# Four stacked graph layers on one core: streamed weights moved to ScalarE's DMA queue, weight combinations spread over phase 1, q's bias folded into a copy, and the planner's order made anew

## The chip, the cores and the metric

The kernel runs on one core of one Trainium2 chip. The metric is the device time of one execution in microseconds. Before the change it is 2448.98 us, the median of two runs (2447.59 and 2450.36).

## What is computed

The input is x (128 graphs of 64 nodes, 512 features, float32) and one 64x64 weighted adjacency per graph. Four layers follow, each as x + layer(relu(layernorm(x))), all in float32:

```python
# layer 0: hypergraph convolution, H = (adj != 0), twice, with a layer norm between
h = layer_norm(relu(hypergraph_conv(h, adj, W1, b1)))      # 512 -> 1024
y = hypergraph_conv(h, adj, W2, b2) + x                    # 1024 -> 512
# layer 1: attention from one score per node, s = (h @ w) @ a
A = exp(lrelu(tanh((s_i + s_j) / 8) * 8)) * adj; A = A / rowsum(A) * rowsum(adj)
out = A @ h @ w
# layer 2: q, k, v attention, masked by adj
weight = adj * exp(q @ k^T); out = (weight / rowsum(weight)) @ v
# layer 3: three hops, H = sum over k of T^k h @ Wk[k] + bk[k], out = relu(H)
T = adj * exp(lrelu(sj + si + ab)); T = T / rowsum(T)
```

## The kernel before

The 8192 nodes are 16 groups of 4 tiles of 128 nodes (two graphs per tile, so a tile's adjacency is block diagonal, buffer tag `bd`). There are two phases. Phase 1 runs layers 0 and 1 over all groups and stores the result to DRAM (`xm`, L845). Phase 2 loads it again and runs layers 2 and 3. The weights of phase 1 lie in SBUF; in phase 2 that memory holds the weights of layer 2 and, in three slots `wf`, pieces of layer 3's weights that are streamed from DRAM.

Matrix products with weights are 2x2 Strassen products with seven multiplications: `seven` (L605 on) multiplies, copies the first partial sum out of PSUM by ScalarE into a buffer U (L612), makes two further sums by VectorE (L614, L616), and hands four results to an `emit` function. `strassen` (L626 on) is used in phase 1, with its matmuls at L644. Layer 2's products (matmuls at L882) go through `seven` too: q first, with the product of Wq and Wk folded into one matrix. `emit_q` gives the four parts of q their bias `gb_c`: the part without U by two ScalarE activations (L896), the three others by a GpSimd addition U + bias (L902) and then a VectorE addition of PSUM (L903). v is made likewise (L936 on GpSimd, L938 on VectorE).

Layer 3 uses two levels of Strassen, so 7 x 7 block products of 128x128, each summed over three hops (matmuls at L1074). The combined weights of each outer product f (7 of them) are made once in phase 1 by `setup_w3` (L517 on): for each f and each hop k (21 calls) it loads blocks of Wk (L525), subtracts on GpSimd (L529, and L533 to L535) and stores the factors to DRAM in `fac` (four stores per call, L539). In phase 2, `product` (L1049 on) reads each f in two parts (768 KB for four blocks, 576 KB for three) into a `wf` slot by a DMA from SyncE (L1066), 14 per group, 224 in all. Results are copied by ScalarE (L1083) or added by VectorE (L1089) into Z, combined by GpSimd (L1097 to L1101), and added to x by VectorE (L1105), then stored (L1109).

Layers 2 and 3 need transposed activations. `transposed` (L588 on) does it with a ScalarE copy (L592), a DMA transpose issued by SyncE (L593), and a ScalarE copy back (L594). Layer norms are VectorE statistics (L553, L554), GpSimd arithmetic (L555, L556, L561) and one ScalarE activation (L574).

The order of all work is made by a planner at build time (`Graph`). Every operation is given an engine, a cost in us, what it reads and writes, and a priority; `run` simulates the engines, and at each step takes the operation that can start first, by priority among equals. A result is ready for others after the operation's cost and the engine's latency (`LATENCY`, 2.0 for DMAs). The priority is `G.prio` plus the shift of the part (`AT`, set by `part`); `step` raises it as work is laid down, by a factor of the layer (`STRETCH`), and a group starts `PERIOD1` or `PERIOD2` after the one before. Where the planner sees TensorE idle for over 0.5 us it puts in filler matmuls (L1141). Each engine then runs its own queue strictly in the planned order, with semaphores for the dependences. All DMAs are issued by SyncE: `dma` makes an operation of engine "SP" with a cost of its size over 380 KB/us, at least 0.34.

Of the kernel before, what the change touches and what calls it, by code (L numbers as in the profile page):

```python
# [35 lines left out]
class Op:  # L36
    __slots__ = ("eng", "cost", "fn", "prio", "bufs", "npre", "succ", "ready", "seq")


class Graph:  # L40
# [11 lines left out]
    def op(self, eng, cost, fn, r=(), w=()):  # L52
        o = Op()
        o.eng, o.cost, o.fn, o.prio = eng, cost, fn, self.prio + self.shift
# [27 lines left out]
    def run(self, slots, after, fill):  # L82
# [22 lines left out]
        while left:  # L105
# [33 lines left out]
            end = t + o.cost + self.LATENCY[o.eng]  # L139
# [28 lines left out]
def tile_adj_preln_d4(  # L168
# [95 lines left out]
    def act(cost, fn, r, w):  # L264
        return G.op("ACT", cost, fn, r, w)
# [4 lines left out]
    def dma(kb, fn, r, w, issue=0.34):  # L270
        return G.op("SP", max(kb / 380.0, issue), fn, r, w)

    def quad(b):
        return b.t.rearrange("p (c k) -> p c k", c=4)

    FILL = 0.75


    STRETCH, PERIOD1, PERIOD2 = (2.6483, 3.2376, 6.9527, 0.0065), 98.8, 156.601
    AT = {  # L280
        "x0": -3298.32, "apart": 470.3, "w1": -1070.96, "b1": -196.66, "w2": 688.02, "w": 1644.63, "c1": 1980.57,
        "l0": 62.93, "c2": -271.12, "l1": -993.03, "c": -522.07, "g0": -2812.96, "g1": -3009.94, "g2": -2266.36,
        "g3": -1918.51, "g": 209.51, "bq": -269.08, "l3": -116.88, "wg": -350.09, "wp": 198.25, "beg0": -729.31,
        "beg1": 4.0, "end00": 12.05, "end01": -60.03, "end11": 292.74, "new2": 91.81, "new3": -3113.8, "end2":
        -59.76, "end3": 2202.11, "load1": -137.15, "load2": 232.55, "m": -67.46, "h0": -22.31, "p0": -73.76, "z0":
        -207.55, "q0": 56.41, "y0": -188.84, "h1": -70.07, "p1": -44.18, "z1": 5.06, "q1": -16.5, "y1": -379.11,
        "s": -93.48, "t0": -481.39, "e0": -248.87, "t1": -22.89, "e1": -398.36, "hT": -2454.84, "sh": -461.03, "lq":
        -187.06, "pt": -94.25, "v": 348.87, "pv": 38.14, "s3": 287.44, "tt": -247.47, "a0": 647.39, "b0": -99.09,
        "a1": 1981.85, "ws": 2277.14, "load3": 1686.98,
    }  # L290

    def part(name):
        G.shift = AT[name]
# [42 lines left out]
    def load_group(g, src, apart=0.0):  # L336
        b = Buf("adj")
        dma(256, lambda: nc.sync.dma_start(b.t, adj[g]), [], [b])
        adjs[g] = b
        for t in range(T):  # L340
            xx = Buf("x")
            at, key = src(g, t)
            G.shift += apart
            dma(256, lambda xx=xx, at=at: nc.sync.dma_start(xx.t, at), key, [xx])
            xt[g, t] = xx
# [30 lines left out]
    gb_c = const.tile([P, KD], F32, name="gb_c")  # L376
    wg_d = dram.tile([D, D], F32, name="wg_d")
# [98 lines left out]
    def setup_bq():  # L476
# [14 lines left out]
        dve(0.2, lambda: nc.vector.tensor_copy(gb_c, pg.t[:, :KD]), [pg], ["gb"])  # L491

# [24 lines left out]
    def setup_w3(f, k):  # L517
# [5 lines left out]
        def load(i, j, key=()):  # L523
            b = Buf("wp")
            dma(256, lambda: nc.sync.dma_start(b.t.rearrange("p (q n) k -> p q (n k)", q=2), src(i, j)), [], [b, *key])  # L525
            return b
# [16 lines left out]
        F = load(*terms[0], turn)  # L543
        for at in terms[1:]:
            Y = load(*at, turn)
            minus(Y, F, F)
# [41 lines left out]
    def transposed(src, ksrc, planes, back, kback, dst, kdst):  # L588
# [4 lines left out]
        dma(0, lambda: nc.sync.dma_start_transpose(u16(back()).rearrange("p (b r) -> p b r", r=P), u16(planes.t)), [planes], kback, 1.23)  # L593
# [11 lines left out]
    def seven(mul, U, n, emit):  # L605
# [6 lines left out]
        act(n / 1200 + 0.17, lambda: nc.scalar.copy(at(0)(), p1.t[:, :n]), [p1], [(U, 0)])  # L612
# [13 lines left out]
    def strassen(A, keys, B, kc, n, stag, emit):  # L626
# [11 lines left out]
        def prod(lhs, kl, b):  # L638
            rhs, kb = B[b]
# [14 lines left out]
        seven({1: prod(a[0, 0], keys[0, 0], "11"), 2: prod(a[0, 1], keys[0, 1], "21"), 3: prod(s4, [(S, 2)], "22"),  # L654
# [69 lines left out]
    def layer0(g):  # L724
# [28 lines left out]
        for t0 in (0, 2):  # L753
# [13 lines left out]
            def emit_z(i, j, p, u, v, t0=t0, zs=zs):  # L767
# [6 lines left out]
                     W1, 2, D, "s1", emit_z)  # L774
# [72 lines left out]
    def layer2(g):  # L847
# [14 lines left out]
        for q, (a, ka, b, kb, op) in enumerate((  # L862
# [4 lines left out]
            dve(c_v(D), lambda q=q, a=a, b=b, op=op: nc.vector.tensor_tensor(X.t[:, q], a(), b(), op), [*ka, *kb], [(X, q)])  # L867
# [24 lines left out]
        def emit_q(i, j, p, u, v):  # L892
# [5 lines left out]
            else:  # L898

                (U, iu), iv = u, v[1]  # L900
                at = lambda: pair(U.t[:, iv])
                pool(1.3, lambda: nc.gpsimd.tensor_add(at(), pair(U.t[:, iu]), gb_c[:, 2 * i:2 * i + 2, None].to_broadcast([P, 2, 2 * P])), [u, "gb"], [v])  # L902
                dve(c_v(D), lambda: nc.vector.tensor_add(at(), pair(p.t), at()), [p], [v])  # L903
                qs.append((i, j, at, [v]))

        seven({n: prod(WG[n], hs[n], True) for n in range(1, 8)}, Buf("u5"), D, emit_q)
# [38 lines left out]
        for t in range(T):  # L945
# [3 lines left out]
            dma(256, lambda xx=xx, at=at: nc.sync.dma_start(xx.t, at), [*key, (PT, 0)], [xx, ("xo", g, t)])  # L949
# [13 lines left out]
    def layer3(g):  # L963
# [39 lines left out]
        for t0 in (0, 2):  # L1003
            part("a0" if t0 == 0 else "a1")
            hh, pqs = [pre_ln(g, t, stats[t]) for t in (t0, t0 + 1)], [[Buf("ps"), Buf("ps")] for _ in range(2)]
            for t, h, b in zip((t0, t0 + 1), hh, a3[t0:t0 + 2]):
                hv = lambda h=h: h.t.rearrange("p (j q k) -> p j q k", j=2, q=2)
                if t >= 2:
                    dve(0.42, lambda hv=hv: nc.vector.tensor_add(hv()[:, 0], hv()[:, 0], hv()[:, 1]), [h], [h])
                if t % 2:  # L1010
                    dve(0.42, lambda hv=hv: nc.vector.tensor_add(hv()[:, :, 0], hv()[:, :, 0], hv()[:, :, 1]), [h], [h])  # L1011
                back = Buf("q")
                transposed(lambda h=h: h.t, [h], Buf("o"), lambda back=back: back.t, [back], lambda b=b: b.t[:, 0], [(b, 0)])
# [28 lines left out]
        def minus(y, x_, blk, kd):  # L1042
            for v in range(2):
                dve(c_v(6 * P), lambda v=v: nc.vector.tensor_sub(blk[v](), y[0][v](), x_[0][v]()), [*y[1][v], *x_[1][v]], [kd[v]])
# [4 lines left out]
        def product(f, F, chain, first):  # L1049
# [7 lines left out]
            dve(c_v(3 * P), lambda: sub(x2(), lo(B), lo(A)), [*ka, *kb], [(X, 0)])  # L1057
            dve(c_v(3 * P), lambda: sub(x3(), hi(B), x2()), [*kb, (X, 0)], [(X, 1)])
            dve(c_v(3 * P), lambda: sub(x4(), hi(A), x2()), [*ka, (X, 0)], [(X, 2)])
            lhs = {1: (lambda: lo(A), ka), 2: (lambda: hi(A), ka), 6: (x2, [(X, 0)]), 5: (lambda: lo(B), kb),  # L1060
                   7: (x3, [(X, 1)]), 3: (x4, [(X, 2)]), 4: (lambda: hi(B), kb)}
            for n in range(2):
# [3 lines left out]
                dma(q * 192, lambda n=n, w_=w_, q=q: nc.sync.dma_start(  # L1066
                    w_.t[:, :q].rearrange("p r k c -> p (r k c)"), fac[f - 1][n]), [("fac", f - 1, n, k, d) for k in range(3) for d in FACS[n]], [w_])
# [23 lines left out]
        def emit(i, j, Z):  # L1091
# [5 lines left out]
            pool(0.8, lambda: add(z(0, 4, 3), z(0, 4, 3), bk3_b[:, 2 * j * P:2 * (j + 1) * P].rearrange("p (a b) -> p a b", a=2)), [(Z, 0), "bk3"], [(Z, 0)])  # L1097
            pool(0.8, lambda: add(z(1, 3), z(1, 3), cast(0)), [(Z, 0)], [(Z, 0)])
            pool(0.8, lambda: add(z(0, 8, 7), z(3, 5), cast(2)), [(Z, 0), (Z, 1)], [(Z, 0), (Z, 1)])
            pool(0.53, lambda: add(z(4, 5), z(7, 8), z(3, 4)), [(Z, 0), (Z, 1)], [(Z, 0), (Z, 1)])  # L1100
            pool(0.8, lambda: add(z(2, 4), z(5, 7), z(0, 8, 7)), [(Z, 0), (Z, 1)], [(Z, 0), (Z, 1)])  # L1101
            cols = slice(2 * j * P, 2 * (j + 1) * P)
            for v in range(2):
                xx = xt[g, 2 * i + v]
                dve(c_v(D // 2), lambda v=v, xx=xx: nc.vector.scalar_tensor_tensor(  # L1105
# [56 lines left out]
    for i in range(21):  # L1162
        G.prio = ((i + 1.0) * (NG - 2.0) / 21) * PERIOD1
        part("wp")
        setup_w3(i // 3, i % 3)
# [89 lines left out]
```

## Time and profile before

| what | value |
|---|---|
| median of the runs | 2448.98 us (2447.59 to 2450.36) |
| the profiled execution | 2453.38 us, span 2450.7 us |
| granted TensorE clock | 0.993 |
| phase 1, steady (366 to 1172 us) | one group in about 73.3 us |
| phase 2, steady (1300 to 2263 us) | one group in about 74.1 us |
| ACT busy in 1300 to 2450.7 | 554.3 us of 1150.7 |
| streamed weights, L1066 | 224 issues, landing 5.0 us (576 KB) and 5.4 us (768 KB), medians |
| DMA transposes, L593 | 256 issues, landing 3.1 to 4.1 us, medians by tile |

All times below are of that one profiled execution. PE is TensorE's matmul stream, PEld its weight loads, DVE VectorE, ACT ScalarE, POOL GpSimd, SP SyncE; "SPq" or "ACTq" is the sequencer of an engine, which waits and issues DMAs while the engine itself is idle. "L616" is line 616 of the kernel. In lists of waits, "A <- B" means that A stood idle until B was done. The window views give, for a stretch, the busy time and count of each engine, then clock, DMA share and GB/s.

### The profile page before, as it was taken

How to read it: one execution, taken by the hardware profiler on the slowest of the kernel's cores; microseconds unless marked ns; L12 is line 12 of the kernel's file. 1: busy time of each engine (PE TensorE's matmuls, PEld its weight loads, DVE VectorE, ACT ScalarE, POOL GpSimd, SP SyncE). 2: the span in 40 equal slices, each digit the busy share in tenths (PEclk: the TensorE clock that was granted, in tenths of full speed). 3: DMA queues.
4: the chain of work that ended last, by engine and by line, in shares of the span. 5: the costliest groups of instructions: out<-in, count | busy, mean ns of one | idle time of the engine just before them, and what ended most of it. 6: DMA issues, size and time to landing. Idle time of an engine off the chain costs nothing.

```text
span 2450.7 us, 39373 instructions
## 1 busy us (share of the span) xinstructions
PE 2335.0 (95%) x14046; PEld 1896.0 (77%) x14046; DVE 1973.5 (81%) x4067; ACT 1320.1 (54%) x1842; POOL 1238.1 (51%) x1822
## 2 busy tenths in 40 slices
PE   7999999999999999999999999999999999999998
PEld 4566677776677776677788888888888988888988
DVE  6888878787778787877778878878888878888886
ACT  3566565665565566565645435554445544445532
POOL 6466665444555444555343535545545545555443
PEclk9999999999999999999999999999999999999999
DMA  8654442322232322233346768767678777688576
GB/s 269 156 135 108 118 118 73 78 60 57 60 74 64 74 61 57 60 75 81 88 130 175 198 184 237 215 181 189 206 218 225 215 184 198 199 234 225 165 217 214
DMA packets 408372, 359.81 MB, mean 147 GB/s; under 512 B 291184, under 2 KB 326768, under 8 KB 408176
## 3 DMA queue, kind: packets, MB, share of 16 engines
q1 hardware_dynamic: 408176, 357.30, 53.7%
q8 instruction: 110, 1.80, 0.3%
q14 instruction: 86, 0.70, 0.1%
HBM read 245.77 MB, written 44.33 MB: 118 GB/s over the span
## 4 chain that ended last, share of the span: by engine, by line
PE 44%; DVE 19%; POOL 14%; DMA 10%; ACT 6%; issue 5%; SPq 1%; POOLq 0%; DVEq 0%; ACTq 0%
PE ps L644 20%; PE ps L1074 9%; PE ps L882 7%; POOL rs L556 3%; PE ps L583 3%; DMA w2m_wm_a_wf<-fac 2%; POOL nm L561 2%; ACT h L574 2%; DVE s_s_zz L636 2%; PE ps L1020 2%; PE ps L795 2%; POOL x L759 2%; DVE st L553 2%; PE ps L953 2%; DMA x<-xm 2%
## 5 line engine op out<-in xcount | busy, mean ns | idle before, releaser
L574 ACT ACTIVATE h<-x,nm,rs 128x512 f32<-128x512 f32 x384 | 300.6, 811 | 295.0 <-POOL nm L561 284.6
L1074 PE MATMUL ps<-w2m_wm_a_wf 128*128 128x128 f32 x2304 | 300.6, 277 | 10.2 <-DMA w2m_wm_a_wf<-fac 4.9
L1074 PEld LDWEIGHTS ps<-w2m_wm_a_wf 128*128 128x128 f32 x2304 | 279.1, 192 | 15.3 <-DMA w2m_wm_a_wf<-fac 4.2
L1074 PE MATMUL ps<-w2m_wm_a_wf,tmp_mB_xi 128*128 128x128 f32 x2016 | 267.0, 278 | 22.5 <-DMA w2m_wm_a_wf<-fac 9.1
L644 PE MATMUL ps<-w2m_wm_a_wf,s_s_zz 128*128 128x256 f32 x1152 | 274.4, 380 | 2.9 <-DVE s_s_zz L636 2.0
L1074 PEld LDWEIGHTS ps<-w2m_wm_a_wf,tmp_mB_xi 128*128 128x128 f32 x2016 | 246.9, 193 | 31.2 <-ACT h L574 15.4
L555 POOL TENSOR_SCALAR rs<-mv 128x1 f32<-128x1 f32 x320 | 104.0, 325 | 323.9 <-DVE mv L554 293.6
L644 PEld LDWEIGHTS ps<-w2m_wm_a_wf,s_s_zz 128*128 128x128 f32 x1152 | 217.2, 190 | 42.8 <-DVE s_s_zz L636 7.0
L644 PE MATMUL ps<-wa_mem,mT_sx 128*128 128x512 f32 x512 | 236.9, 597 | 7.2 <-DVE u L616 5.8
L644 PE MATMUL ps<-w2m_wm_a_wf,rT_wp_vu_tt 128*128 128x256 f32 x1024 | 240.3, 380 | 3.5 <-ACT u L612 2.1
L644 PEld LDWEIGHTS ps<-w2m_wm_a_wf,rT_wp_vu_tt 128*128 128x128 f32 x1024 | 191.0, 190 | 43.4 <-issue 11.2
L556 POOL TENSOR_TENSOR rs<-rs,mhalf 128x1 f32<-128x1 f32 x320 | 210.0, 656 | 25.6
L553 DVE BATCH_NORM_STATS2 st<-x 128x6 f32<-128x512 f32 x256 | 174.8, 683 | 16.1 <-DMA x<-xm 10.5
L644 PEld LDWEIGHTS ps<-wa_mem,mT_sx 128*128 128x128 f32 x512 | 96.7, 191 | 114.3 <-issue 98.0
L644 PE MATMUL ps<-wa_mem,s_s_zz 128*128 128x512 f32 x384 | 178.8, 594 | 3.7 <-DVE s_s_zz L636 2.3
L672 POOL TENSOR_TENSOR u<-u,row_sh 128x256 f32<-128x256 f32 x96 | 76.9, 813 | 189.8 <-DVE u L614 138.0
L592 ACT COPY o<-h 128x1024 uint16<-128x1024 uint16 x128 | 133.6, 1043 | 48.1 <-DVE h L1011 43.2
L561 POOL TENSOR_SCALAR nm<-mv,rs 128x1 f32<-128x1 f32 x320 | 141.4, 442 | 31.4
L594 ACT COPY rT_wp_vu_tt<-z_hT 128x1024 uint16<-128x1024 uint16 x128 | 145.5, 1161 | 13.5 <-DMA z_hT<-tmp_mB_xi 13.4
L836 POOL TENSOR_TENSOR x<-x,u 128x256 f32<-128x256 f32 x96 | 80.1, 851 | 143.4 <-DVE u L616 119.8
L583 PEld LDWEIGHTS ps<-bd,h 128*128 128x128 f32 x1024 | 129.7, 192 | 28.5 <-issue 17.6
L644 PEld LDWEIGHTS ps<-wa_mem,s_s_zz 128*128 128x128 f32 x384 | 72.3, 190 | 89.1 <-issue 77.7
(187 smaller groups left out, 5182.7 us busy)
## 6 DMA issues: line engine op xcount, KB each, us to landing
w2m_wm_a_wf<-fac SPq DMA_DIRECT2D x112, 768.0 KB, 5.4
w2m_wm_a_wf<-fac SPq DMA_DIRECT2D x112, 576.0 KB, 5.0
x<-xm SPq DMA_DIRECT2D x128, 256.0 KB, 3.9
x<-in_x_dram SPq DMA_DIRECT2D x64, 256.0 KB, 2.8
xm<-x SPq DMA_DIRECT2D x64, 256.0 KB, 2.1
out_dram<-x SPq DMA_DIRECT2D x64, 256.0 KB, 3.8
rT_wp_vu_tt<-in_Wk_dram SPq DMA_DIRECT2D x42, 256.0 KB, 3.0
adj<-in_adj_dram SPq DMA_DIRECT2D x32, 256.0 KB, 4.1
```

What stands on the lines that cost most here:

```text
L553: dve(0.69, lambda i=i: nc.vector.bn_stats(st.t[:, i, :], src(i)), [r[i]], [(st, i)])
L555: pool(0.32, lambda: nc.gpsimd.tensor_scalar_add(rs.t, mv.t[:, 1:2], EPS), [mv], [rs])
L556: pool(0.65, lambda: nc.gpsimd.tensor_tensor(rs.t, rs.t, mhalf, ALU.pow), [rs], [rs])
L561: pool(0.47, lambda: nc.gpsimd.tensor_scalar(nm.t, mv.t[:, 0:1], rs.t, -1.0, op0=ALU.mult, op1=ALU.mult), [mv, rs], [nm])
L574: act(0.82, lambda: nc.scalar.activation(h.t, xx.t, AF.Relu, bias=nm.t, scale=rs.t), [xx, nm, rs], [h])
L583: nc.tensor.matmul(quad(p)[:, c, :], h.t[:, c * P:(c + 1) * P], rhs(), start=True, stop=True)
L592: act(1.05, lambda: nc.scalar.copy(u16(planes.t).rearrange("p (q c) -> p q c", q=2), u16(src()).rearrange("p (c q) -> p q c", q=2)), ksrc, ...
L594: act(1.16, lambda: nc.scalar.copy(u16(dst()).rearrange("p c (k q) -> p c k q", q=2), u16(back()).rearrange("p (q c r) -> p c r q", q=2, c ...
L644: nc.tensor.matmul(p.t[:, :n], lhs()[:, c, :], rhs(c), start=first and c == 0, stop=c == kc - 1, skip_group_check=True)
L836: pool(0.75, lambda: nc.gpsimd.tensor_add(xx.t[:, cols], xx.t[:, cols], U.t[:, iu]), [xx, u], [xx])
L882: nc.tensor.matmul(pair(p.t)[:, o, :], a, b, start=first and o == 0 and c == 0, stop=c == 1, skip_group_check=True)
L1074: nc.tensor.matmul(inner(p, q)[:, r, :], at()[:, k, :], w_.t[:, r, k, :], start=first and r == 0 and k == 0, stop=k == 2, skip_group_check ...
```

## The change

Five edits:

1. The streamed weights (L1066) are issued by ScalarE (`nc.scalar.dma_start`) and not by SyncE. In the plan they are a ScalarE operation of cost 0.1 and latency 4.8, where they were a SyncE operation of cost 2.02 or 1.52 and latency 2.0.
2. The 21 calls of `setup_w3`, which had priorities spread over phase 1 but no dependence, are laid down two per group, at the end of each group, and their first load waits for the group's first store to `xm`.
3. q's bias: the first copy of `seven` out of PSUM becomes two ScalarE activations that add the bias of rows i=1, so that the sums made from it hold it already. The GpSimd additions L902 go. For i=1, VectorE adds PSUM and U; for i=0 two VectorE instructions of half the width add PSUM, U and the difference of the biases, `gb_d`, made once.
4. The planner gets a latency per operation, and several costs are changed (VectorE's combinations of layer 2 and 3, GpSimd's output chain, landings of x and of the transposes). `strassen` names the buffers U and `outs` as needed by its first product; this is seen by the planner alone.
5. All shifts, stretches and periods are new, so that every engine's order is new.

```diff
-    def op(self, eng, cost, fn, r=(), w=()):
+    def op(self, eng, cost, fn, r=(), w=(), lat=None):
         o = Op()
+        o.lat = self.LATENCY[eng] if lat is None else lat
...
-            end = t + o.cost + self.LATENCY[o.eng]
+            end = t + o.cost + o.lat
...
-    STRETCH, PERIOD1, PERIOD2 = (2.6483, 3.2376, 6.9527, 0.0065), 98.8, 156.601
+    FILL, LAT = 0.75, 2.6
+    STRETCH, PERIOD1, PERIOD2 = (3.062, 0.5167, 15.0185, 0.0052), 97.433, 148.006
...
-        "a1": 1981.85, "ws": 2277.14, "load3": 1686.98,
+        "v": 150.08, "pv": -967.75, "s3": 201.11, "tt": 163.32, "a0": 211.94, "b0": -128.64, "a1": 233.51, "ws":
+        -2004.09, "load3": 10.36,
...
+        dve(0.16, lambda: nc.vector.tensor_sub(gb_d, gb_c[:, 0:2], gb_c[:, 2:4]), ["gb"], ["gbd"])
...
-    def setup_w3(f, k):
+    def setup_w3(f, k, when):
...
-        F = load(*terms[0], turn)
+        F = load(*terms[0], when)
...
-        dma(0, lambda: nc.sync.dma_start_transpose(u16(back()).rearrange("p (b r) -> p b r", r=P), u16(planes.t)), [planes], kback, 1.23)
+        dma(0, lambda: nc.sync.dma_start_transpose(u16(back()).rearrange("p (b r) -> p b r", r=P), u16(planes.t)), [planes], kback, 1.23, lat)
...
-    def seven(mul, U, n, emit):
+    def seven(mul, U, n, emit, first=None):
...
-        act(n / 1200 + 0.17, lambda: nc.scalar.copy(at(0)(), p1.t[:, :n]), [p1], [(U, 0)])
+        if first:
+            first(p1)
+        else:
+            act(n / 1200 + 0.17, lambda: nc.scalar.copy(at(0)(), p1.t[:, :n]), [p1], [(U, 0)])
...
-                at = lambda: pair(U.t[:, iv])
-                pool(1.3, lambda: nc.gpsimd.tensor_add(at(), pair(U.t[:, iu]), gb_c[:, 2 * i:2 * i + 2, None].to_broadcast([P, 2, 2 * P])), [u, "gb"], [v])
-                dve(c_v(D), lambda: nc.vector.tensor_add(at(), pair(p.t), at()), [p], [v])
+                at, at0 = (lambda: pair(U.t[:, iv])), (lambda: pair(U.t[:, iu]))
+                if i:
+                    dve(c_v(D), lambda: nc.vector.tensor_add(at(), pair(p.t), at0()), [p, u], [v])
+                else:
+                    for o in range(2):
+                        dve(0.48, lambda o=o: nc.vector.scalar_tensor_tensor(
+                            at()[:, o], pair(p.t)[:, o], gb_d[:, o:o + 1], at0()[:, o], op0=ALU.add, op1=ALU.add), [p, u, "gbd"], [v])
...
+        def first(p):
+            for o in range(2):
+                act(0.46, lambda o=o: nc.scalar.activation(pair(U.t[:, 0])[:, o], pair(p.t)[:, o], AF.Identity, bias=gb_c[:, 2 + o:3 + o]), [p, "gb"], [(U, 0)])
...
-                dma(q * 192, lambda n=n, w_=w_, q=q: nc.sync.dma_start(
-                    w_.t[:, :q].rearrange("p r k c -> p (r k c)"), fac[f - 1][n]), [("fac", f - 1, n, k, d) for k in range(3) for d in FACS[n]], [w_])
+                act(0.1, lambda n=n, w_=w_, q=q: nc.scalar.dma_start(
+                    w_.t[:, :q].rearrange("p r k c -> p (r k c)"), fac[f - 1][n]), [("fac", f - 1, n, k, d) for k in range(3) for d in FACS[n]], [w_], 4.8)
...
-            pool(0.8, lambda: add(z(1, 3), z(1, 3), cast(0)), [(Z, 0)], [(Z, 0)])
+            pool(0.92, lambda: add(z(1, 3), z(1, 3), cast(0)), [(Z, 0)], [(Z, 0)])
...
-    for i in range(21):
-        G.prio = ((i + 1.0) * (NG - 2.0) / 21) * PERIOD1
-        part("wp")
-        setup_w3(i // 3, i % 3)
     for g in range(NG):
...
             layer(g)
+        G.prio = (g + 1.0) * PERIOD1
+        part("wp")
+        for i in range(2 * g, min(2 * g + 2, 21)):
+            setup_w3(i // 3, i % 3, [("xmid", g, 0)])
```

## The prediction

> **What bounds the kernel now.** I read the page, then the windows by stage, then the waits, then one stall in the timeline. The windows give span, then busy time and count of PE, PEld, DVE, ACT and POOL, the clock, the DMA share and GB/s.
>
> ```profile
> PE 2335.0 (95%) x14046; PEld 1896.0 (77%) x14046; DVE 1973.5 (81%) x4067; ACT 1320.1 (54%) x1842; POOL 1238.1 (51%) x1822
> ...
> q1 hardware_dynamic: 408176, 357.30, 53.7%
> ```
>
> ```profile
> 0.00:146.00 146.00, 128.49 (x432) 74.08 (x432) 112.64 (x220) 75.36 (x106) 84.40 (x123) 0.95 0.70 199
> 146.00:366.00 220.00, 213.79 (x895) 151.10 (x895) 179.11 (x370) 128.88 (x178) 147.91 (x217) 1.00 0.47 118
> 366.00:1172.00 806.00, 794.41 (x3336) 571.65 (x3335) 643.01 (x1396) 492.96 (x685) 394.50 (x627) 1.00 0.29 68
> ...
> 1300.00:2263.00 963.00, 903.77 (x7217) 833.01 (x7216) 797.35 (x1590) 482.68 (x674) 481.41 (x671) 0.99 0.73 206
> ```
>
> TensorE sets the time everywhere, and only its holes can be won. In steady phase 1 they are 11.6 us of 806 (1.4%): next to nothing. In steady phase 2 they are 59.2 of 963 (6.1%), in the start (0 to 366) 23.7. The whole run has 2450.7 - 2335.0 = 115.7. All DMAs ride on one queue, q1, issued by SP. What ends PE's waits in phase 2 (us in total, times, longest), what SP's queue waits for, and the cost of issuing a streamed weight on SP (min/median/max ns):
>
> ```profile
> PEld ps L882 <- DVE u L616: 24.7, 12, 2.7
> ...
> PEld ps L1074 <- ACT h L574: 15.4, 10, 2.3
> ...
> PE ps L1074 <- DMA w2m_wm_a_wf<-fac: 14.2, 13, 2.1
> ```
>
> ```profile
> SPq L1066 <- PE ps L1074: 261.6, 150, 14.6
> ...
> SPq L1066 <- DMA w2m_wm_a_wf<-fac: 23.3, 15, 2.3
> ```
>
> ```profile
> L1066 SPq DMA_DIRECT2D w2m_wm_a_wf<-fac x224: 319/326/1196, 1277.9 to 2435.8; - x112
> ```
>
> The largest wait once, in the timeline of a middle group. DVE stands behind POOL's output chain (L1101) with its additions L1105; the partial sum L616 that PE needs is queued behind them, and PE waits 2.21 us:
>
> ```profile
> 1889.09 0.73 POOL L1101 TENSOR_TENSOR s_s_zz<-s_s_zz 128x256 f32<-128x256 f32 x1
> ...
> 1889.85 1.58 DVE L1105 SCALAR_TENSOR_TENSOR x<-s_s_zz,x 128x256 f32<-128x256 f32 x2 [0.55 <-POOL s_s_zz L1101]
> ...
> 1891.36 0.68 DVE L616 TENSOR_TENSOR u<-ps,u 128x512 f32<-128x512 f32 x1
> ...
> 1892.09 1.13 PE L882 MATMUL ps<-row_sh,wa_mem 128*128 128x256 f32 x4 [2.21 <-DVE u L616]
> ```
>
> **What the Trainium skill says.** "DMA: Bandwidth & Descriptors", section "Issuing engines are not separate DMA queues": DMAs from scalar and sync run on the same 16 engines and interleave; a second issuer saves only the sequencer's issue time. So no bandwidth is gained; the trace's 0.73 DMA share in phase 2 stays. Same page, "Queues, rings and completion order": SP and ACT each own a ring on every DMA engine, and an engine goes round-robin over its rings by packet. So a weight no longer stands behind a transpose, nor a transpose behind a weight; they share instead. No run yet shows two rings here. "Perfetto Trace Analysis", "DMA Instruction — HWDGE (DVE, Sync)": the issuing sequencer is held until the descriptors are made; L1066 agrees with its 326 ns median. "SBUF — State Buffer", "Who interferes with whom": DVE with two SBUF inputs and GpSimd contend for a shared port. The trace agrees: L1059 takes 0.55 us at 1864.48 and 1.09 at 1801.32, where POOL's L1099 runs until 1801.99, so POOL work removed also shortens DVE.
>
> **The change part by part**, against the profiled execution (run 2453.4, span 2450.7; the median of the runs is 2449.0, so differences are carried over to it).
>
> *Weights to ScalarE's queue.* 224 issues leave SP: 224 x 0.326 = 73 us, with 261.6 + 23.3 = 285 us of waits in front of everything SP has queued behind (transposes L593, x loads, stores). They come to ACT: 73 us more beside 554 us busy in 1300 to 2451, and up to 285 us of waits for PE to release a slot, behind which stand h (L574), snapshots (L1083), transposes' copies (L592, L594). The planner counts 0.1 us for an issue, so some 0.23 x 224 = 51 us are unplanned. What of that reaches PE? ACT ended about 28 us of PEld's waits in 1300 to 2263 (15.4 + 4.7 + 4.4 + 2.0 + 1.8) with 483 us of work, 6%. 6% of 73 + 285 = 21 us if its new waits count like work, 4 if only the issue does. I take +10; the ends are 0 (ACT half idle) and the rival below. Gain: weights are asked for as soon as a slot is free (part "ws" goes from +2277 to -2004), planned with a landing of 4.8 us where it was 2.0 after 1.5 to 2.0 of issue; measured 5.0 to 5.4. PE's waits for weights are 14.2 + 4.2 (PEld) = 18.4. I take -14; ends -18 and +20 (a landing of 5.2 against two other slots' 4.7 us of matmuls, short by about 0.8 us wherever three products follow each other).
>
> *q's bias.* 48 POOL additions L902 go (48 x 1.06 = 50.9 us of POOL; DVE waited 12.7 us for them). The first copy becomes two 128x256 activations like L896, 467 ns each: 934 instead of 581, +0.35 x 16 = 5.6 us of ACT, at worst all of it before PE's next product; one of three sums becomes two of 128x256 like L959, 479 ns each: 958 instead of 687, +4.3 us of DVE in total. Both lie beside PE's products (1.73 us each). Net at nothing by themselves, +6 to -12; they matter through the next term.
>
> *Costs that the planner now knows.* POOL's chain L1097 to L1101 was planned at 0.8/0.53 and runs at 0.82 to 0.96/0.64; the new costs are 0.84 to 0.92/0.64; L867, L1044, L1009 likewise; landings LAT 2.6. The L616 stall comes from that chain being late, and recurs in 12 groups: with the chain planned late, and L902 gone from the same queue, L616 should go ahead of L1105. I take -22 of 24.7. Of the other waits in phase 2 of the same kind (ACT h 15.4, z_hT 4.4, snapshots 4.7, DVE L938 6.3, L990 4.8), 36 us, the new order should take some 40%: -14, ends 0 and -30.
>
> *Combinations spread.* POOL's 27.9 + 17.4 + 13.1 + 12.8 = 71 us and 42 loads and 84 stores leave the first 370 us for two per group after each group's xm store: 6.5 us more POOL per group on 49% busy, and 11 to 12 issues of 0.37 us on SP. Holes in 0 to 366 above the steady rate: 23.7 - 5.3 = 18.4 us. I take half, -9. Cover for the moved work: POOL's and SP's idle time; gone, SP's waits at L539 and L525 (94 us) would stand before phase 1's transposes: 0 to +10.
>
> *Bookkeeping.* `outs` and `lat` issue no instruction. The order of everything else is new and cannot be read from the diff: -15 to +15.
>
> Sum: +10 - 14 + 0 - 22 - 14 - 9 = -49: 2449 - 49 = **2400 us**.
>
> **The rivals.**
> Stalls move on. DVE is 83% busy and DMA 73% in phase 2; PE's hole closes in one place and opens in another (weights and transposes now slow each other, PE waits at L1074 for fac or at L882 for z_hT). Only the start's -9 stays: about 2440. For it: 13 of the 17 causes in PE's list for phase 2 are under 5 us each. Against: two causes alone make 43 us.
>
> As good a plan as phase 1's. PE's holes in phase 2 fall to 1.4%: the 74.1 us of 1300 to 2451 become 16, -58; with the start -14: about 2377. For it: phase 1 shows that this planner can do it. Against: phase 1 has DMA at 0.29 and far fewer short matmuls.
>
> Slower: ScalarE blocked behind PE. Its queue is in order, and a weight's issue waits for the slot that PE frees; mean 358/224 = 1.6 us with the issue. Where the next ACT instruction is one that PE needs soon (a snapshot that frees a bank, h), PE is late by that. Without other gains than the start's, PE pays 1.6 us for each such issue: over 2% slower (+49) needs (49 + 9)/1.6 = 36 of 224, or 67 with all gains kept. At 45 with no gain: 2449 - 9 + 72 = about 2512. For it: 150 of 224 issues did wait on SP. Against: ACT's own waits show that it follows PE already (L1083, L1025, L1001), and half its time is free.
>
> **How the numbers follow.** Likeliest 45% (2378 to 2424); stalls move 22% (2420 to 2465); plan as in phase 1 12% (2350 to 2385); slower 21% (from 2480 to 2560, a little below). Two per cent, about what a measurement of this kernel can tell from no change, is 49 us: the line is 2400, through the middle of the likeliest. Faster 0.45 x 0.5 + 0.12, rounded to 0.35; within 2% 0.44; slower 0.21. The range 2350 to 2480 leaves out most of the slower case.
>
> **What would show it.** Right: a second hardware queue with 150 MB; L902 gone; the wait L882 <- L616 under 5 us; PE <- fac under 6; PE's holes in steady phase 2 at about 3% instead of 6.1; DMA share in 0 to 366 down and spread to about 850 us. Wrong: the weight issues on ACT's queue waiting over 250 us for PE, with PE's waits ended by ACT rising over 60; PE <- fac rising with landings above 6 us; new holes in the start. The prediction fails first if the two-queue landing is far from 5 us, or ACT's issues cost PE more than 10.

## The result and the profile after

The kernel after takes 2598.28 us, the median of two runs (2593.73 and 2602.82), where the kernel before takes 2448.98: a ratio of 1.061, 95% interval 1.0526 to 1.0693. The change makes the kernel about 149 us slower. The profiled execution took 2593.73 us, its span is 2591.9 us, its mean granted TensorE clock 0.967 (before 0.993).

Below are three lines of the page of the kernel after: the engines' busy time, and the two DMA queues with packets, MB and share of 16 engines' span.

```profile
PE 2399.4 (93%) x14190; PEld 1951.4 (75%) x14190; DVE 1968.2 (76%) x4084; ACT 1331.6 (51%) x1858; POOL 1182.5 (46%) x1774
...
q1 hardware_dynamic: 375920, 203.15, 33.6%
q10 hardware_dynamic: 32256, 154.16, 20.1%
```

The edits are all there: the second queue carries the weights, GpSimd is busy 56 us less (1182.5 for 1238.1), ScalarE and VectorE do what they did. But PE's holes, span less busy time, rose from 115.7 to 192.5 us, and PE itself is busy 64 us longer with only 144 instructions more. The windows of the kernel after say where (span, busy time and count of PE, PEld, DVE, ACT and POOL, then clock, DMA share, GB/s):

```profile
0.00:366.00 366.00, 351.35 (x1422) 238.70 (x1423) 296.91 (x613) 213.70 (x297) 179.03 (x277) 1.00 0.41 109
366.00:1172.00 806.00, 783.35 (x3284) 560.53 (x3283) 657.73 (x1364) 484.83 (x668) 455.06 (x683) 1.00 0.35 86
1300.00:2263.00 963.00, 854.55 (x6510) 782.72 (x6509) 682.77 (x1421) 433.80 (x612) 380.54 (x563) 0.93 0.72 182
```

The start is fuller than before (14.7 us of holes for 23.7), steady phase 1 a little emptier (22.7 for 11.6). All the loss is in steady phase 2: holes of 108.5 us of 963 for 59.2, a clock of 0.93 for 0.99, 6510 PE instructions for 7217. The DMA share is the old one, 0.72 for 0.73, yet the engines move 182 GB/s for 206: as busy, with less done.

The waits of the kernel after (engine, line, what it waited for: us in total, times, longest):

```profile
ACT w2m_wm_a_wf L597 <- DMA wa_q<-o: 240.3, 44, 15.8
...
ACT z_hT L597 <- DMA h<-o: 117.3, 44, 10.0
...
DVE ee L720 <- DMA rw<-row: 74.8, 16, 9.4
...
PE ps L930 <- DVE u L911: 50.7, 11, 7.3
...
PE ps L888 <- ACT z_hT L597: 33.2, 13, 4.0
...
PE ps L1089 <- DMA w2m_wm_a_wf<-fac: 12.9, 9, 4.6
```

L597 is the copy back after a DMA transpose (L594 before), L888 layer 2's products (L882 before), L1089 layer 3's (L1074 before), L930 the logits. The same copy in the kernel before:

```profile
ACT w2m_wm_a_wf L594 <- DMA wa_q<-o: 104.4, 31, 7.5
...
ACT z_hT L594 <- DMA h<-o: 61.9, 42, 3.5
```

The stall on the partial sum (L616 before, L622 now) is gone from PE's long waits, as forecast. In its place ScalarE waits for these transposes 357.6 us (166.3 before), and PE waits for what is late behind that: z_hT, and the logits' operand u (L911). The new queue's own row, from the view of line L1081 of the kernel after, looks harmless (min/median/max):

```profile
L1081 ACTq DMA_DIRECT2D w2m_wm_a_wf<-fac x224: 325/326/447, 1280.1 to 2576.0; - x112
...
DMA to landing us min/median/max: 3.6/5.3/13.7
```

The median landing is 5.3 us, near what the plan (4.8) and the prediction (5.2) assumed. The trouble is in the tail, 13.7 us, and transposes and row loads that are in flight at the same time land late too. Here is the largest wait once, in the timeline of the kernel after (start, duration, engine, line):

```profile
1779.94 1.15 SPq L692 DMA_DIRECT2D rw<-row  x2
1780.05 3.01 ACTq L1081 DMA_DIRECT2D w2m_wm_a_wf<-fac  x2
...
1781.19 12.11 SPq L596 DMA_TRANSPOSE wa_q<-o  x2
...
1786.70 0.61 DVE L720 TENSOR_TENSOR ee<-rw,col 128x256 f32<-128x256 f32 x1 [4.27 <-DMA rw<-row]
...
1790.89 1.16 ACT L597 COPY w2m_wm_a_wf<-wa_q 128x1024 uint16<-128x1024 uint16 x1 [10.83 <-DMA w2m_wm_a_wf<-fac]
1791.95 0.41 ACT L990 ACTIVATE ee<-ee 128x256 f32<-128x256 f32 x1
...
1792.39 0.43 DVE L991 TENSOR_TENSOR ee<-ee,adj 128x256 f32<-128x256 f32 x1 [3.68 <-ACT ee L990]
...
1793.61 0.85 DVE L911 SCALAR_TENSOR_TENSOR u<-ps,gb_d,u 128x256 f32<-128x256 f32 x2
...
1794.11 1.04 PE L930 MATMUL ps<-u,z_hT 128*64 128x64 f32 x16 [4.67 <-DVE u L911]
```

Two weights (ScalarE's ring) and a transpose (SyncE's ring) start within 2.7 us. By the trace the transpose of 1781.19 lands at 1790.86, after 9.7 us, and the copy L597 that reads it starts 0.03 us later, having held ScalarE for 10.83 us (the profile names a weight here, which comes in beside it; 44 other waits of L597, 240.3 us, are put down to the transpose itself). The small row load `rw` lands after 6.1 to 6.4 us and holds VectorE for 4.27. Behind L597 in ScalarE's order stands an exponential (L990) that has nothing to do with the transpose; VectorE's next operation L991 waits for it; behind that on VectorE stands L911; and PE waits 4.67 us for L911. A late DMA passes through three in-order queues before it reaches PE.

### The profile page after: what moved, and what is told of

Same layout as the page of the kernel before. It is cut to its first block, busy times and chain, and to the rows that moved or that the text cites. A ratio compares the mean times of both kernels' runs of the same rounds, so it can differ in the third digit from the quotient of the medians.

```text
span 2591.9 us, 39722 instructions
## 1 busy us (share of the span) xinstructions
PE 2399.4 (93%) x14190; PEld 1951.4 (75%) x14190; DVE 1968.2 (76%) x4084; ACT 1331.6 (51%) x1858; POOL 1182.5 (46%) x1774
## 3 DMA queue, kind: packets, MB, share of 16 engines
q10 hardware_dynamic: 32256, 154.16, 20.1%
## 4 chain that ended last, share of the span: by engine, by line
PE 40%; DVE 21%; DMA 19%; ACT 7%; POOL 7%; issue 5%; SPq 1%; ACTq 0%; DVEq 0%; POOLq 0%
PE ps L650 17%; PE ps L888 8%; DMA wa_q<-o 6%; PE ps L1089 6%; DMA h<-o 6%; PE ps L586 3%; DVE s_s_zz L642 2%; DVE o L383 2%; DVE st L556 2%; DVE u L668 2%; DMA row<-col 2%; DMA adj<-in_adj_dram 2%; PE ps L1035 2%; PE ps L968 2%; POOL rs L559 2%
## 5 line engine op out<-in xcount | busy, mean ns | idle before, releaser
L1089 PE MATMUL ps<-w2m_wm_a_wf 128*128 128x128 f32 x2304 | 300.8, 277 | 3.8 <-DMA w2m_wm_a_wf<-fac 2.5
L558 POOL TENSOR_SCALAR rs<-mv 128x1 f32<-128x1 f32 x320 | 109.9, 343 | 403.2 <-DVE mv L557 389.8
L1089 PEld LDWEIGHTS ps<-w2m_wm_a_wf 128*128 128x128 f32 x2304 | 282.7, 193 | 7.8 <-issue 2.2
L1089 PE MATMUL ps<-w2m_wm_a_wf,tmp_mB_xi 128*128 128x128 f32 x2016 | 273.4, 283 | 10.5 <-DMA w2m_wm_a_wf<-fac 10.4
L1089 PEld LDWEIGHTS ps<-w2m_wm_a_wf,tmp_mB_xi 128*128 128x128 f32 x2016 | 256.3, 199 | 16.6 <-issue 5.1
L650 PEld LDWEIGHTS ps<-w2m_wm_a_wf,rT_wp_vu_tt 128*128 128x128 f32 x1024 | 192.3, 190 | 35.9 <-issue 10.3
L597 ACT COPY w2m_wm_a_wf<-wa_q 128x1024 uint16<-128x1024 uint16 x64 | 74.4, 1162 | 251.3 <-DMA wa_q<-o 240.3
L650 PE MATMUL ps<-wa_mem,s_s_zz 128*128 128x512 f32 x384 | 181.9, 598 | 13.2 <-DVE s_s_zz L642 11.9
L597 ACT COPY rT_wp_vu_tt<-z_hT 128x1024 uint16<-128x1024 uint16 x128 | 145.7, 1159 | 23.5 <-DMA z_hT<-tmp_mB_xi 23.0
L1114 POOL TENSOR_TENSOR s_s_zz<-s_s_zz 128x256 f32<-128x256 f32 x64 | 58.0, 906 | 208.1 <-DVE s_s_zz L1104 154.9
L788 ACT ACTIVATE z_hT<-z_hT,nm,rs 128x512 f32<-128x512 f32 x128 | 103.5, 812 | 94.7 <-POOL nm L564 94.4
```

Of the source, the lines that this page charges most:

```text
L558: pool(0.32, lambda: nc.gpsimd.tensor_scalar_add(rs.t, mv.t[:, 1:2], EPS), [mv], [rs])
L597: act(1.16, lambda: nc.scalar.copy(u16(dst()).rearrange("p c (k q) -> p c k q", q=2), u16(back()).rearrange("p (q c r) -> p c r q", q=2, c ...
L650: nc.tensor.matmul(p.t[:, :n], lhs()[:, c, :], rhs(c), start=first and c == 0, stop=c == kc - 1, skip_group_check=True)
L788: act(0.72, lambda half=half, rs=rs, nm=nm: nc.scalar.activation(half(), half(), AF.Identity, bias=nm.t, scale=rs.t), [(z, j), rs, nm], [( ...
L1089: nc.tensor.matmul(inner(p, q)[:, r, :], at()[:, k, :], w_.t[:, r, k, :], start=first and r == 0 and k == 0, stop=k == 2, skip_group_check ...
```

## The experiments

Theory after this result: **two rings**. Bulk weights on one ring beside transposes and small loads on the other make these land late. Rivals: **ScalarE blocked** (the prediction's slow case: issues in ScalarE's queue wait for slots), and **the new order** itself (the planner's shifts, or the combinations in phase 1).

### One line each: the ring alone, in both orders

The new order with the weights on SyncE's ring, at the same place in the plan, and the old order with them on ScalarE's ring:

```diff
# e1, from the kernel after (L1081)
-                act(0.1, lambda n=n, w_=w_, q=q: nc.scalar.dma_start(
+                act(0.1, lambda n=n, w_=w_, q=q: nc.sync.dma_start(
# e2, from the kernel before (L1066)
-                dma(q * 192, lambda n=n, w_=w_, q=q: nc.sync.dma_start(
+                dma(q * 192, lambda n=n, w_=w_, q=q: nc.scalar.dma_start(
```

Expected of the first:

> The changed kernel with its order kept on every engine, but the 224 weight loads issued by SyncE (on the one ring) at the same place of the order. Two rings as the cause (weights in 6 KB rows share each DMA engine packet by packet with the transposes' small packets and starve them): the transposes for layer 3 (wa_q) land in 4.3 us on average again instead of 6.3, the small row loads in 3.4 instead of 6.7, and the time falls to 2430 to 2500. The order as the cause (weights asked for at the first moment, up to three in flight, planned as if they took no bandwidth): the transposes stand behind the same weights in the one ring, land no sooner, and the time stays at 2560 to 2640.

It took 2432.32 us, ratio to the kernel before 0.9933 (0.991 to 0.9956): 166.0 us less than the kernel after, by one word, and 18.5 us less than the kernel before (2450.81 in that comparison). Steady phase 1 and 2 in its windows (columns as above):

```profile
366.00:1172.00 806.00, 781.63 (x3287) 560.43 (x3287) 658.09 (x1370) 480.51 (x666) 455.15 (x678) 1.00 0.35 85
1300.00:2263.00 963.00, 931.00 (x7540) 860.16 (x7541) 786.63 (x1649) 497.96 (x701) 439.45 (x643) 1.00 0.75 209
```

The holes of phase 2 are 32.0 us of 963 (59.2 before, 108.5 after), the clock is back at 1.00, and 209 GB/s flow. Phase 1, where no weight is streamed, is as in the kernel after: what is emptier there is the order, not the ring. Its waits:

```profile
ACT w2m_wm_a_wf L597 <- DMA wa_q<-o: 180.0, 45, 9.8
...
ACT z_hT L597 <- DMA h<-o: 83.0, 48, 4.8
...
PE ps L1014 <- DVE rT_wp_vu_tt L1005: 12.8, 13, 1.8
...
PE ps L1089 <- DMA w2m_wm_a_wf<-fac: 10.3, 13, 1.3
...
PE ps L888 <- ACT z_hT L597: 7.1, 5, 3.7
```

The PE lines are the first, third and fifth of PE's list: no cause holds PE's matmuls for more than 13 us in the whole run. ScalarE still waits 263.0 us for transposes here, 97 more than before, and yet the kernel is faster than before: the total of these waits is not what costs. What fell against the kernel after is the longest of them (9.8 us for 15.8, 4.8 for 10.0) and what reaches PE (7.1 us for 33.2 at L888). `wa_q` lands after 4.57 us in the mean and the row loads after 4.32 (6.29 and 6.65 after, 4.33 and 3.38 before): much earlier, though not all the way back to the 4.3 and 3.4 that were expected.

Expected of the second:

> The kernel before with its order kept, but the 224 weight loads issued by ScalarE on a second ring. Two rings as the cause: landings of wa_q rise above 5.5 us on average and the time to 2520 or more. The order as the cause: landings stay near 4.3 and the time within 2430 to 2480. ScalarE held by its issues (my slower rival of the prediction): PE's waits ended by ScalarE rise from some 30 us to over 60 and the time to over 2500 with landings unchanged.

It took 2562.38 us, ratio 1.0469 (1.0441 to 1.0497), 112 us more than the kernel before, with the order before. In its waits the new leader is the same copy:

```profile
PE ps L882 <- ACT z_hT L594: 65.9, 13, 7.2
...
PE ps L1074 <- DMA w2m_wm_a_wf<-fac: 20.3, 22, 2.7
```

The time is what the two-ring theory expected; which transpose suffers is not what was expected of it: here `h` lands late (3.64 to 5.28 us in the mean, 10.0 at the 90th percentile), while `wa_q` moves only from 4.33 to 4.52. Which one is hit may depend on which meets the weights in time; that was not followed up.

This run alone does not part the two theories: PE's waits that ScalarE ended rose over 60 us too, which was the sign of ScalarE being held by its issues. Against that stands that `h` lands later. And I worked out from the trace how long a weight's issue stood waiting after the instruction ahead of it on its own queue was done: 298 us on SyncE before, 121.9 us on ScalarE after, but only 39.8 us in this run, which is 112 us slower than before all the same. The new order falls as the cause of the loss: with the order kept, one line moves the time by 166 us in the new order and by 112 in the old.

### How late things land

Means that I worked out from the traces, in us: landing less start of issue, all of phase 2 (after 1240 us); the start of the last store to `xm`; and us per group over groups 2 to 12:

```text
kernel (weights on / transposes on)   last xm store  us/group  wa_q   h     rows  weights
before      (SyncE / SyncE)               1282         74.40   4.33  3.64  3.38   5.21
after       (ScalarE / SyncE)             1281         85.71   6.29  4.69  6.65   5.90
e1          (SyncE / SyncE)               1288         72.45   4.57  3.98  4.32   5.57
e2          (ScalarE / SyncE), old order  1279         81.43   4.52  5.28  3.59   5.54
e6          (ScalarE / ScalarE)           1350         75.09   5.55  3.84  6.21   5.84
e7          (SyncE / ScalarE)             1350         82.52   6.76  4.65  6.61   6.05
e8          (ScalarE / SyncE), short rows 1291         81.96   5.66  4.84  5.67   6.55
e9          (SyncE / SyncE), short rows   1293         75.70   4.71  4.50  4.18   6.23
```

"Rows" are the `rw` loads. In each pair with the same order, two rings give the longer period: 85.7 for 72.5, 81.4 for 74.4, 82.5 for 75.1, 82.0 for 75.7.

### The meeting measured by itself

This kernel computes none of the layers. Eight times for each variant it issues a DMA transpose and three 768 KB loads in a given order and from given queues, with a wait between the bursts: alone; on one ring with the transpose first (1tfirst) or last (1wfirst); on two rings (2rings); on two rings with a single load (2one); on two rings with the loads in 512-byte rows (2short).

```python
if what == "t":
    nc.sync.dma_start_transpose(u16(h).rearrange("p (b r) -> p b r", r=P), u16(o))
else:                       # three loads, from nc.sync or nc.scalar
    ring.dma_start(dst(ws[n]), src(n))
```

> Not the layers (it computes none of the output): the disputed cost by itself. Eight variants, each eight times from rest: one transpose of 128x512 float32 alone; three weight loads of 768 KB alone; transposes issued just ahead of three weights, and just behind, on SyncE's one ring; transpose on SyncE with three weights, and with one, on ScalarE's ring at the same moment; three weights in rows of 512 bytes alone, and on ScalarE's ring beside the transpose. Two rings as the cause, packet by packet: ahead of the weights on one ring the transpose lands as alone (about 3 us); on two rings it lands with the weights (8 to 12 us with three, 4 to 5.5 with one); with weights in short rows it suffers less than with long ones. If two rings by themselves do nothing, it lands in about 3 to 4 us in all but the variant behind the weights.

Its DMA issues, with the median us from issue to landing last (h is the transpose, w the loads):

```profile
wwalone<-in_Wk_dram SPq DMA_DIRECT2D x24, 768.0 KB, 6.3
w1tfirst<-in_Wk_dram SPq DMA_DIRECT2D x24, 768.0 KB, 6.5
w1wfirst<-in_Wk_dram SPq DMA_DIRECT2D x24, 768.0 KB, 5.9
w2rings<-in_Wk_dram ACTq DMA_DIRECT2D x24, 768.0 KB, 9.0
wshortalone<-in_Wk_dram ACTq DMA_DIRECT2D x24, 768.0 KB, 7.9
w2short<-in_Wk_dram ACTq DMA_DIRECT2D x24, 768.0 KB, 7.8
...
w2one<-in_Wk_dram ACTq DMA_DIRECT2D x8, 768.0 KB, 4.8
htalone<-otalone SPq DMA_TRANSPOSE x8, 3.0
h1tfirst<-o1tfirst SPq DMA_TRANSPOSE x8, 3.1
h1wfirst<-o1wfirst SPq DMA_TRANSPOSE x8, 8.6
h2rings<-o2rings SPq DMA_TRANSPOSE x8, 12.9
h2one<-o2one SPq DMA_TRANSPOSE x8, 5.8
h2short<-o2short SPq DMA_TRANSPOSE x8, 6.5
```

A transpose alone lands after 3.0 us. Behind three loads on its own ring it takes 8.6 (its issue starts 1.3 to 1.4 us after theirs). On the other ring, beside them, 12.9: later than if it had queued behind all of them. The loads suffer too (9.0 for 5.9 to 6.5 on one ring), so this is not only a matter of who goes first. A burst of three loads and a transpose, from first issue to last landing, takes 9.8 to 10.6 us on one ring in all 16 cases and 10.3 to 17.4 us on two, 13.2 in the median: throughput is lost. Beside a single load the transpose takes 5.8, which is still 2.8 more than alone, and the load 4.8. Both figures are a little over what was expected (at most 12 and 5.5).

Beside loads in short rows the transpose takes 6.5, and these loads are not slowed (7.8 for 7.9 alone). This variant is less clean than the others: a load waits for its own buffer only, so in seven of the eight bursts the loads began 2.5 to 5.1 us ahead of the transpose. In the one burst from rest it took 6.3, where the first burst with long rows took 10.2.

The single packets in the trace show how the two share the engines. In the seven bursts of the two-ring variant where loads and transpose began together, from the fifth to the eighth us after the transpose's issue, 46 of its packets (256 bytes each) move per us and 34 of the loads' (6 KB each). With one ring, 61 packets of the loads move per us in the third to sixth us after the first load's issue with the weights first, and the transpose alone has moved all its 1024 in about 1.4 us. So the two go nearly packet for packet, and both are slowed.

### The two rings exchanged

All DMA transposes go to ScalarE's ring too, so that there is one ring for both, while x, stores and row loads stay on SyncE's (e6); and the same with the weights on SyncE's, two rings with the roles exchanged (e7):

```diff
-        dma(0, lambda: nc.sync.dma_start_transpose(...), [planes], kback, 1.23, lat)
+        dma(0, lambda: nc.scalar.dma_start_transpose(...), [planes], kback, 1.23, lat)
# e7 has the edit of e1 besides
```

> The changed kernel with its order kept, weights on ScalarE's ring as in the change, and all DMA transposes issued by ScalarE too, so that both are on one ring again; ScalarE is held by some 256 x 1.24 = 317 us of transposes' issues more. Two rings between weights and transposes as the cause: wa_q lands in about 4.6 us on average, as in the same order on one ring, and the time is clearly under that of the next run. ScalarE held by its queue as the cause of the loss: slower than the changed kernel, 2620 or more, and slower than the next run.

> The changed kernel with its order kept, weights issued by SyncE and all DMA transposes by ScalarE: two rings again, with the roles exchanged; ScalarE never waits for a weight's slot. Two rings as the cause: wa_q and h land late again (means over 4.7 and 6 us) and the time is 2540 or more. ScalarE held by weights as the cause: landings as on one ring, and the time well under 2540.

The first took 2535.21 us, ratio 1.0346 (1.0312 to 1.0379); the second 2627.68, ratio 1.0714 (1.0663 to 1.0765). Both lose time in phase 1, where no weight is streamed: the last store to `xm` comes at 1350 us, for 1281 after and 1288 in e1. The 128 transposes of phase 1 now take 1.25 us of ScalarE each for their issue, 160 us in all, and land as before (median 3.1 us); this hold of ScalarE is the likely reason, but it was not tried apart. From there they part: 92 us by the weights' ring alone, with the same order. In e7 ScalarE issues no weight, so it cannot wait for a weight's slot, and yet it is the slower of the two. The waits of e7 show the signature of the kernel after:

```profile
PE ps L888 <- ACT z_hT L597: 34.6, 13, 4.8
```

In e6 the same wait is 8.1 us. So "ScalarE blocked by the weights" falls as the cause of the loss in phase 2. Two figures missed: with both on one ring, `wa_q` landed after 5.55 us in the mean, where 4.6 was expected; and in e7 the two means are 6.76 (`wa_q`) and 4.65 (`h`), where over 4.7 and 6 was expected, so that the lower one stayed just under. The row loads, still on SyncE's ring beside weights on the other, stayed late in e6 (6.21).

### Row length

The loads of the kernel after and of e1, with `fac` laid out block by block so that a weight arrives in rows of 512 bytes and not of 4.5 or 6 KB:

```diff
-    fac = [[dram.tile([P, n * 3 * P], F32, ...) for n in (4, 3)] for f in range(7)]
+    fac = [[dram.tile([n * 3, P, P], F32, ...) for n in (4, 3)] for f in range(7)]
```

> The changed kernel, its order and its two rings kept, but the factors lie in DRAM block by block, so that a weight load is made of rows of 512 bytes instead of 6144 or 4608. If the rings share each DMA engine packet by packet, the transposes suffer less: wa_q's mean landing falls from 6.3 to 5.5 us or less, while a weight itself lands later (7 us or more, as it does alone); the loss against the same with one ring (next run) is under 90 us where it is 166 with long rows. If the length of the rows doesn't matter, the loss stays near 166.

> The same short rows with the weights issued by SyncE on the one ring, in the same order: the control of the run before it. Weights land 1.5 to 2 us later than with long rows and their issue holds SyncE longer, so slower than the long rows on one ring by 20 to 120 us under every theory.

On two rings 2564.09 us, ratio 1.0462 (1.0445 to 1.0479); on one 2484.79, ratio 1.0137 (1.012 to 1.0154). The short rows cost 52 us on one ring and win 34 on two; the ring's price falls from 166 to 79 us. Row length matters, and by half. `wa_q` at 5.66 and the weights at 6.55 us are a little outside what was expected (at most 5.5, at least 7), and on one ring the weights land 0.7 us later than with long rows, not 1.5 to 2.

### The other parts

q's bias alone in the old order: the two activations and the one-instruction sums of the change, GpSimd's additions left out, every other instruction where it was.

```diff
-                pool(1.3, lambda: nc.gpsimd.tensor_add(at(), pair(U.t[:, iu]), ...), [u, "gb"], [v])
+                pool(1.3, lambda: None, [u, "gb"], [v])
...
+        def first(p):
+            for o in range(2):
+                nc.scalar.activation(pair(U.t[:, 0])[:, o], pair(p.t)[:, o], AF.Identity, bias=gb_c[:, 2 + o:3 + o])
```

> The kernel before with edit 3 alone and its order kept: two activations with bias in the place of the first copy, no GpSimd addition L902, the sums as in the change. As the prediction priced it the bias itself is between -12 and +6 us and the wait of layer 2's matmuls for L616 may shrink from 24.7: 2420 to 2455. If the bias were part of the loss (the logits of the changed kernel wait for its half-width sums): over 2470.

2437.27 us, ratio 0.9943 (0.9928 to 0.9958): 13.5 us faster. Its wait for the partial sum is 13.7 us on PE and 18.4 on PEld:

```profile
PEld ps L886 <- DVE u L620: 18.4, 12, 1.9
...
PE ps L886 <- DVE u L620: 13.7, 11, 1.5
```

Before, these were 20.1 and 24.7. VectorE's wait for L902, 12.7 us before, is gone with the 48 additions; its wait for GpSimd's output chain (L1101) hardly moved, 23.8 us for 24.3. By which of its steps the edit shortened the stall is not shown.

The kernel after, with the weights given back to SyncE in the plan too, at the old cost and latency, and everything planned anew with the new shifts:

```diff
-                act(0.1, ... nc.scalar.dma_start(... [w_], 4.8)
+                dma(q * 192, ... nc.sync.dma_start(... [w_])
```

> The changed kernel with edit 1 alone undone: weights are a SyncE operation with the old cost and latency, planned anew with the new shifts. Both theories of the weights: the time goes back to 2420 to 2480. If the rest of the change (shifts, costs, bias, combinations) is the cause, it stays above 2550.

2533.8 us, ratio 1.0335 (1.032 to 1.0351): a miss for everything expected of it. It has one ring, and its transposes land in time (4.44 us), so the ring is not its trouble. PE waits for weights 30.2 us in 28 places and a group takes 81.0 us. The shifts were made for a weight that the plan asks for early and counts at 4.8 us of latency; with another model of the same transfer they give another order, and that order is worse: 101 us slower than e1, with the same ring and the same other edits. Which part of it loses was not followed up. So planned anew, the other edits cannot be told from the plan, and e1 with its order kept is the clean comparison. The spread of the combinations was not tried alone.

## Why the prediction was wrong, by its own steps

**Weights to ScalarE's queue** is the step that failed. The prediction took from the Trainium skill ("DMA: Bandwidth & Descriptors", "Issuing engines are not separate DMA queues") that a second issuer saves only the sequencer's time, and from "Queues, rings and completion order" there that an engine serves its rings in turn by packet; and it read this as neutral: "they share instead". It gave the sharing no term in its sum; +20 was the worst end under "weights -14". Its rival "stalls move on" did name the mechanism ("weights and transposes now slow each other", PE waiting for z_hT), but priced it as no more than the gains lost, about 2440. Measured by e1 against the kernel after, the sharing costs +166 us, and by e2 against before +112. The first section agrees with the runs in that no bandwidth is gained; that nothing is lost, which I read into it, no run shows, and e5 shows the contrary. The second agrees: in e5 the two rings move 46 and 34 packets per us, nearly one for one, and a turn is worth 256 bytes to the transpose and 6 KB to a load, so turns by packet favour the weights; short rows halve the loss, as that would have it. But turns alone don't make the transpose later than behind all three loads, nor bring the loads from 61 packets per us to 34, so part of the cause stays open.

The error can be traced further. The prediction named nearly the right symptom ("the two-queue landing is far from 5 us") but did not say of which landings: its figures were medians of the weights, and that median is 5.3; the mean of the weights went to 5.90 and of the row loads to 6.65, from 5.21 and 3.38. And it listed what moves with the weights without asking what is left on the other ring and who stands behind it: transposes, on which ScalarE waits in order.

**+10 for ScalarE's issues.** An issue costs 326 ns as taken. ScalarE's issues stood behind finished work for 121.9 us, not 285 and not over 250. The slower rival had the right sign and about two fifths of the loss (2512, +63 of +149), by the wrong mechanism: ScalarE is blocked, but by late transposes (357.6 us of waits at L597, up to 15.8 at a time), not by slots that PE frees late. e7 shows that it happens with no weight in its queue.

**PE's clock** was no term at all. PE is busy 2399.4 us in the kernel after and 2341.4 us in e1, with the same 14190 instructions: 58.0 of the 161.8 us between their spans; the holes are the other 103.8 (192.5 for 88.7). The slower PE goes with the lower granted clock, 0.93 for 1.00 in steady phase 2.

**Weights, -14.** In e1, asked for early on SyncE's ring, PE's waits for weights at L1089 are 10.3 us for 14.2. The 18.4 that the -14 was taken from counted most of PEld's 4.2 twice, since they lie almost wholly within PE's 14.2 (14.8 together); 4.5 of the 14 came.

**q's bias, 0 (ends -12 and +6).** -13.5 in the old order, just past its end. The working had it right that this acts in part through the next term: the stall on the partial sum shrinks with it, by 6.4 us on PE.

**The L616 stall -22, other waits of phase 2 -14.** In e1 the stall is gone, and a group takes 72.45 us for 74.40: 16 groups make -31 for all terms in phase 2 together. These two and the weights' -14 had -50 (the +10 for ScalarE's issues does not apply in e1). In the old order q's bias alone takes a group to 73.35, which makes -17. So the direction held at about three fifths of the size, and if the parts add, which was not tried, more than half of that is q's bias and the planner's new costs are worth little. The -22 was also more than the hole: 24.7 is the wait of the weight load, PE's own was 20.1.

**Start and spread, -9.** Group 0 is done 14 us earlier in the kernel after and 11 in e1 (170 and 173 for 184 us), then each of the next ten groups takes 75.0 (75.4 in e1) instead of 73.5 us, about as long as the combinations last; the last store to `xm` comes at 1281 and 1288 for 1282. The gain is given back: -1 to +6. That the cover, idle GpSimd and SyncE in steady phase 1, was not free would explain it, but the order is new too, and the two were not parted.

All edits but the ring, as e1 has them, are worth -18.5 us where -49 was summed for the whole, and the ring, which was to be worth little, +166. The lowest time is that of e1, the change with its weights left on SyncE's ring, 0.9933 (0.991 to 0.9956) of the kernel before; q's bias alone, 0.9943 (0.9928 to 0.9958), cannot be told from it. Both are clear of no change by their intervals, but within the 2% that the prediction drew as its line.

## What to carry to other kernels

In a kernel like this one, keep bulk loads and the small, urgent DMAs (transposes above all) on one ring and order them there: a transpose ahead of three loads landed after 3.1 us, behind them after 8.6. Before moving a stream to another queue, ask what it will overlap with and which in-order engine stands behind the one that becomes late. Judge landings by their mean and tail, not only by their median, and try the ring alone first: it is one word, with the order kept. Shifts tuned for one planner's model can lose their worth when a cost or a latency in it changes, as e3 shows.

## What the runs showed of the hardware

A DMA transpose beside three 768 KB loads on another ring lands after 12.9 us, against 8.6 behind them on the same ring and 3.0 alone, and the burst as a whole takes 13.2 us for 10.0. With one load beside it is 5.8, with three in 512-byte rows 6.5. While both rings are at work, 46 packets of the transpose and 34 of the loads move per us, where 61 of the loads move on one ring. The busy share of the DMA engines doesn't show the loss: 0.72 in steady phase 2 with 182 GB/s, 0.75 with 209. Issued by ScalarE, a transpose holds it for 1.25 us; with all of them there, phase 1 ended 62 to 69 us later. And holes of 11% in PE's stretch went with a granted clock of 0.93, holes of 3% with 1.00.
